# Taking a graph network's transposes off TensorE: VectorE's 32x32 blocks and a way through memory

## The chip, the cores and the metric

One core of one Trainium2 chip. The metric is the time of one execution in device microseconds (us), as the median of several runs.

## The reference, cut to what matters

Thirty-two independent graphs ("batches") of 512 nodes with 128 features pass through four residual layers. Each layer normalizes x, takes ReLU, and adds what a graph layer makes of it.

```python
x   = (32, 512, 128) float32;  adj = (32, 512, 512) float32
h = relu(layernorm(x));  x = x + L0(h)   # degree-normalized aggregation over adj + I
h = relu(layernorm(x));  x = x + L1(h)   # three projections, aggregations over adj and its transpose, update, tanh
h = relu(layernorm(x));  x = x + L2(h)   # four such layers in a row; rows and columns of adj scaled to unit length
h = relu(layernorm(x));  x = x + L3(h)   # one message and a gated update
```

A projection contracts over features and needs h with features on the partitions; a normalization runs over features and needs nodes on the partitions. So each batch turns a 512x128 block round four times: h into hT for L1, h into f0 for L2, L2's result f back into rows (added to x), and h into hT for L3.

## The kernel before

Every operation is put into a plan: an engine, an estimated duration, what it reads and writes. A list scheduler (`Plan.order`) plays the plan through with these estimates and so fixes the order of instructions on each engine. On the chip each engine takes its instructions in that order, and waits only for what it needs. The estimates decide nothing else. About three batches are under way at a time.

```python
PERIOD = 25.0          # a batch is due this much after the one before it (only sets priorities)
SMALL = 8              # how many buffers of each small kind go round
...
class Plan:
    SIGNAL = {"PE": 0.24, "DVE": 0.16, "ACT": 0.17, "POOL": 0.1, "SP": 0.05, "AQ": 0.05}
    ...
    def t_pow(n):      # planned us of a reciprocal root on GpSimd over n columns
        return 0.9 + 0.1 * n
...
        def normed(xin, out_tag, extra=None):
            v8 = buf("v8", (P, 2 * NC)); n = NC
            mv = moments(xin, v8)                 # VectorE; v8 = variance + eps
            if extra: extra(v8); n = 2 * NC       # first norm of a batch: the degrees too, 8 columns
            inv = buf("sc", (P, 3 * NC))
            op("POOL", t_pow(n), lambda: nc.gpsimd.tensor_tensor(inv[:, :n], v8[:, :n], neg_half[:, :n], op=ALU.pow), ...)
            ...
            op("DVE", 0.08, lambda: nc.vector.scalar_tensor_tensor(nb, mv[:, :, 0], -1.0, inv[...], mult, mult), ...)
            for c in range(NC):                   # ScalarE: h = relu(x * inv + nb), four blocks
                op("ACT", ..., lambda c=c: nc.scalar.activation(h[:, c, :], xin[:, c, :], AF.Relu, bias=nb[...], scale=inv[...]), ...)

        def transposed(h, name):                  # three of the four turnings
            ps = plan.bank("t")
            for c in range(NC):
                op("PE", 0.11, lambda c=c: nc.tensor.transpose(ps[:, c*P:(c+1)*P], h[:, c, :], ident), ...)
            hT = buf("s2", name=name)
            op("ACT", t_act(N), lambda: nc.scalar.copy(hT, ps), ...)
            return hT
...
        # layer 0: adj + I, only the diagonal blocks, on GpSimd (two SBUF inputs)
            nc.gpsimd.tensor_tensor(diag[:, k:k+n, :], blocks_of_aT, ident, op=ALU.add)
...
        # layer 2: adj and its transpose times the reciprocal lengths, 8 VectorE instructions of 128x512 per batch
        for s, m in enumerate((aT, a)):
            for c in range(NC):
                op("DVE", 1.0, lambda: nc.vector.tensor_mul(m[:, c, :], m[:, c, :], rows[:, :, s, :]), ...)   # two SBUF inputs
...
        pst = plan.bank("t")                      # the fourth turning
        for c in range(NC):
            op("PE", 0.11, lambda c=c: nc.tensor.transpose(pst[:, c*P:(c+1)*P], f[0][:, c*P:(c+1)*P], ident), ...)
        tt(x3, lambda: nc.vector.tensor_add(x3, x2, pst), ...)
```

## Time and profile before

| | before |
|---|---|
| time, median of 3 | 2416.8 us (2416.28 to 2417.7) |
| span of the profile | 2415.3 us |
| TensorE busy | 99%, 8898 matmuls, 512 of them transposes |
| VectorE / ScalarE / GpSimd busy | 49% / 33% / 12% |

The measure used throughout is the **step**: the time from one TensorE instruction's start to the next one's. Each group of equal matmuls has a median step; count times median, summed, is the floor, what TensorE needs if nothing is ever late (2355.6 us). What the steps have above it is the stall (38.4 us, of which 16.4 between 100 and 2300 us, "mid-run").

### The profile page before, as it was taken

How to read it: one execution, taken by the hardware profiler on the slowest of the kernel's cores; microseconds unless marked ns; L12 is line 12 of the kernel's file. 1: busy time of each engine (PE TensorE's matmuls, PEld its weight loads, DVE VectorE, ACT ScalarE, POOL GpSimd, SP SyncE). 2: the span in 40 equal slices, each digit the busy share in tenths (PEclk: the TensorE clock that was granted, in tenths of full speed). 3: DMA queues.
4: the chain of work that ended last, by engine and by line, in shares of the span. 5: the costliest groups of instructions: out<-in, count | busy, mean ns of one | idle time of the engine just before them, and what ended most of it. 6: DMA issues, size and time to landing. Idle time of an engine off the chain costs nothing.

```text
span 2415.3 us, 23480 instructions
## 1 busy us (share of the span) xinstructions
PE 2379.2 (99%) x8898; PEld 1464.4 (61%) x8898; DVE 1195.2 (49%) x2855; ACT 790.1 (33%) x1719; POOL 299.0 (12%) x218
## 2 busy tenths in 40 slices
PE   6999999999999999999999999999999999999998
PEld 4566566656665665666566656656665666666565
DVE  7445445545445454455554454544555545555423
ACT  5213333333333333333333333333333333333312
POOL 2001111111111111111111111111111111111001
PEclk9999999999999999999999999999999999999999
DMA  6002221022211122210222111222102221122100
GB/s 250 31 1 70 70 70 44 27 70 70 70 50 31 60 70 70 70 44 27 70 70 70 46 32 62 70 70 70 44 27 70 70 70 44 31 66 70 48 5 9
DMA packets 95441, 139.67 MB, mean 58 GB/s; under 512 B 8160, under 2 KB 41312, under 8 KB 95328
## 3 DMA queue, kind: packets, MB, share of 16 engines
q1 hardware_dynamic: 95040, 138.04, 17.4%
q8 instruction: 70, 1.15, 0.2%
q14 instruction: 43, 0.35, 0.0%
q10 hardware_dynamic: 288, 0.13, 0.0%
HBM read 129.64 MB, written 8.52 MB: 57 GB/s over the span
## 4 chain that ended last, share of the span: by engine, by line
PE 86%; DVE 8%; POOL 3%; ACT 2%; issue 0%; DMA 0%; SPq 0%; POOLq 0%; DVEq 0%
PE ps_agg L284 54%; PE ps_sd L284 18%; PE ps_gate L284 7%; PE ps_upd L284 3%; POOL sc L400 3%; PE ps_t L420 2%; DVE rep L524 1%; PE ps_msg L284 1%; PE ps_lin L284 1%; DVE aT L568 1%; DVE bn L384 1%; DVE sd L455 1%; DVE rep L522 1%; ACT h L412 1%; DVE node L517 1%; DVE xr L594 1%
## 5 line engine op out<-in xcount | busy, mean ns | idle before, releaser
L284 PE MATMUL ps_agg<-aT,sd 128*128 128x512 f32 x1024 | 517.1, 592 | 0.0
L284 PE MATMUL ps_agg<-a,sd 128*128 128x512 f32 x1024 | 516.8, 592 | 0.0
L284 PE MATMUL ps_sd<-w_sb,f 128*128 128x256 f32 x1792 | 488.5, 381 | 1.5 <-ACT f L585 0.8
L455 DVE TENSOR_TENSOR sd<-ps_sd,rf_sb 128x512 f32<-128x512 f32 x256 | 176.3, 689 | 557.1 <-PE ps_sd L284 553.8
L284 PEld LDWEIGHTS ps_sd<-w_sb,f 128*128 128x128 f32 x1792 | 325.7, 191 | 206.9 <-issue 179.9
L400 POOL TENSOR_TENSOR sc<-v,neg_half 128x4 f32<-128x4 f32 (+1 forms) x128 | 196.2, 1533 | 1457.6 <-DVE v L387 1015.6
L412 ACT ACTIVATE h<-xr,nb,sc 128x128 f32<-128x128 f32 x384 | 161.4, 484 | 374.8 <-DVE nb L408 374.7
L284 PEld LDWEIGHTS ps_agg<-a,sd 128*128 128x128 f32 x1024 | 185.0, 190 | 108.8 <-issue 99.5
L284 PEld LDWEIGHTS ps_agg<-aT,sd 128*128 128x128 f32 x1024 | 187.4, 191 | 104.4 <-issue 85.2
L585 ACT ACTIVATE f<-ps_agg,cf_sb 128x512 f32<-128x512 f32 x128 | 87.4, 683 | 439.4 <-PE ps_agg L284 439.4
L284 PE MATMUL ps_agg<-f,w_sb 128*128 128x512 f32 x448 | 229.7, 594 | 0.0
L619 DVE TENSOR_TENSOR g<-ps_gate,r_sb 128x512 f32<-128x512 f32 x128 | 83.4, 684 | 128.3 <-PE ps_gate L284 128.3
L568 DVE TENSOR_TENSOR aT<-aT,rows 128x512 f32<-128x512 f32 x128 | 134.9, 1077 | 3.2 <-PE ps_agg L284 3.0
L284 PE MATMUL ps_agg<-aT,rep 128*128 128x512 f32 x256 | 132.8, 600 | 0.5 <-DVE rep L524 0.5
L568 DVE TENSOR_TENSOR a<-a,rows 128x512 f32<-128x512 f32 x128 | 132.1, 1086 | 2.5 <-PE ps_agg L284 2.5
L284 PE MATMUL ps_agg<-a,rep 128*128 128x512 f32 x256 | 130.7, 592 | 0.0
L284 PE MATMUL ps_agg<-aT,msg 128*128 128x512 f32 x256 | 129.8, 592 | 0.0
L284 PEld LDWEIGHTS ps_agg<-f,w_sb 128*128 128x128 f32 x448 | 84.9, 191 | 73.4 <-issue 62.2
L455 DVE TENSOR_TENSOR sd<-ps_sd,r_sb 128x512 f32<-128x512 f32 x64 | 44.3, 691 | 151.2 <-PE ps_sd L284 151.2
L548 ACT ACTIVATE sq<-aT 128x512 f32<-128x512 f32 x128 | 80.6, 630 | 81.1 <-DMA aT<-in_adjt 78.2
L480 POOL TENSOR_TENSOR diag<-aT,ident 128x512 f32<-128x512 f32 (+1 forms) x35 | 41.4, 1182 | 508.7 <-DMA aT<-in_adjt 441.5
L420 PEld LDWEIGHTS ps_t<-ident,h 128*128 128x128 f32 x384 | 51.9, 141 | 84.1 <-ACT h L412 45.1
(94 smaller groups left out, 2751.0 us busy)
## 6 DMA issues: line engine op xcount, KB each, us to landing
aT<-in_adjt SPq DMA_DIRECT2D x63, 1024.0 KB, 7.7
a<-in_adj SPq DMA_DIRECT2D x31, 1024.0 KB, 6.9
rows<-bounce SPq DMA_DIRECT2D x32, 512.0 KB, 4.1
x<-in_x SPq DMA_DIRECT2D x32, 256.0 KB, 6.2
out<-xo SPq DMA_DIRECT2D x30, 256.0 KB, 2.5
raw<-in_raw SPq DMA_DIRECT2D x2, 768.0 KB, 7.5
a<-in_adj SPq DMA_DIRECT2D x4, 256.0 KB, 6.2
aT<-in_adjt SPq DMA_DIRECT2D x4, 256.0 KB, 6.0
```

Source lines behind the costliest of these rows:

```text
L284: op("PE", t_mm(n), lambda: nc.tensor.matmul(out_of(ps.ap()), lhs(), rhs(), start=start, stop=stop), reads, [(ps, part) if part is not Non ...
L384: op("DVE", 0.193, lambda c=c: nc.vector.bn_stats(st.ap()[:, c, :], xin.ap()[:, c, :]), [xin], [(st, {c})])
L400: op("POOL", t_pow(n), lambda: nc.gpsimd.tensor_tensor(inv.ap()[:, :n], v8.ap()[:, :n], neg_half[:, :n], op=ALU.pow), [v8, NH], [(inv, {0})])
L412: op("ACT", t_act(D, 2), lambda c=c: nc.scalar.activation(h.ap()[:, c, :], xin.ap()[:, c, :], AF.Relu, bias=nb.ap()[:, c:c + 1], scale=inv ...
L420: op("PE", 0.11, lambda c=c: nc.tensor.transpose(ps.ap()[:, c * P:(c + 1) * P], h.ap()[:, c, :], ident), [(h, {c}), ID], [(ps, {c})])
L455: op("DVE", t_tt(N), lambda ps=ps, h=h: nc.vector.tensor_add(sd.ap()[:, 2 * h:2 * h + 2, :], ps.ap().rearrange("p (j v) -> p j v", j=2), a ...
L480: nc.gpsimd.tensor_tensor(diag.ap()[:, k:k + n, :], blocks, ident[:, None, :].to_broadcast([P, n, P]), op=ALU.add)
L517: tt(node, lambda: nc.vector.tensor_max(node.ap(), zn.ap(), en.ap()), N, [zn, en])
L548: op("ACT", 0.73, lambda c=c, s=s, m=m: nc.scalar.activation(sq.ap(), m.ap()[:, c, :], AF.Square, accum_out=stat.ap()[:, s * NC + c:s * NC ...
L568: op("DVE", 1.0, lambda m=m, c=c, s=s: nc.vector.tensor_mul(m.ap()[:, c, :].rearrange("p (k n) -> p k n", k=NC), m.ap()[:, c, :].rearrange ...
L585: op("ACT", t_act(N, 1), lambda ps=ps, i=i, f_new=f_new: nc.scalar.activation(f_new.ap(), ps.ap(), AF.Tanh, bias=cf_sb[:, i:i + 1]), [ps, ...
L619: op("DVE", t_tt(N), lambda ps=ps, c=c: nc.vector.tensor_add(g.ap()[:, c, :], ps.ap(), r_sb[:, R_L3_G:R_L3_G + 4 * D]), [ps, RS], [(g, {c})])
```

## The change

The intent is to take 432 of TensorE's 512 transposes away, since TensorE is the bound. In batches 3 to 29 VectorE transposes the 32x32 blocks of the tile, four DMA writes put the blocks at their places in device memory, and one DMA reads the turned tile back. The planner's constants are set anew as well.

```diff
-PERIOD = 25.0
+PERIOD = 30.0
-SMALL = 8
+SMALL = 16
-    SIGNAL = {"PE": 0.24, "DVE": 0.16, "ACT": 0.17, "POOL": 0.1, "SP": 0.05, "AQ": 0.05}
+    SIGNAL = {"PE": 0.2, "DVE": 0.13, "ACT": 0.14, "POOL": 0.0, "SP": 0.05, "AQ": 0.05}
+    LOAD = 0.1                      # and lag() adds LOAD when the next operation is TensorE's
-    plan = Plan(..., {"bank": 1, "s2": 7, "s4": 1, "s8": 1})
+    plan = Plan(..., {"bank": 1, "s2": 7, "s4": 0, "s8": 0})
+        def turned(m, name):
+            blk, mT = buf("s2", rows_shape, "blk"), buf("s2", rows_shape, name)
+            op("DVE", t_tt(N), lambda: nc.vector.transpose(<blk, column blocks swapped>, <m, in 32-column blocks>), [m], [blk])
+            bounce = buf(f"turn_{name}", rows_shape)
+            for k in range(NC):
+                op("SP", 0.4, lambda k=k: away(k), [blk], [(bounce, {k})], kb=64)       # 32 partitions each
+            op("SP", 0.4, lambda: nc.sync.dma_start(mT.ap(), bounce.tile), [bounce], [mT], kb=256)
+            return mT
+        at_ends = b < 3 or b >= B - 2
         def transposed(h, name):
+            if at_ends: <as before>
+            t, hT = turned(h, "turned"), buf("s2", name=name)
+            op("ACT", t_act(N), lambda: nc.scalar.copy(hT..., turned_cols(t)), [t], [hT])
-        op("POOL", 5.5, lambda: <root of the row lengths>, ...)
+        op("POOL", t_pow(2 * NC), lambda: <root of the row lengths>, ...)
-        <fourth turning on TensorE, added to x2 from PSUM>
+        <if at_ends as before, otherwise f4 = turned(f[0], "f4r") and added to x2 from there>
```

More of the change, by code (lines that the diff above doesn't have):

```diff
@@ L142, in lag @@
         queued = o.engine == n.engine and o.engine in self.RESULT
-        return o.us + self.RESULT[o.engine] if queued else o.us + o.land + self.SIGNAL[o.engine]
+        if queued:
+            return o.us + self.RESULT[o.engine]
+        return o.us + o.land + self.SIGNAL[o.engine] + self.LOAD * (n.engine == "PE")
     def order(self):
@@ L235, in gnn_stack @@
     dram = ctx.enter_context(tc.tile_pool(name="dram", bufs=1, space=bass.MemoryType.DRAM))
-    plan = Plan(sb, psum, {"bank": 8, "s2": 32, "s4": 6, "s8": 10}, {"bank": 1, "s2": 7, "s4": 1, "s8": 1})
+    plan = Plan(sb, psum, {"bank": 8, "s2": 32, "s4": 6, "s8": 10}, {"bank": 1, "s2": 7, "s4": 0, "s8": 0})
     w_sb = const.tile([P, W_COLS], F32, name="w_sb")
@@ L415, in normed, with away, turned_cols @@
             return h, inv
-        def transposed(h, name):
-            ps = plan.bank("t")
-            for c in range(NC):
-                op("PE", 0.11, lambda c=c: nc.tensor.transpose(ps.ap()[:, c * P:(c + 1) * P], h.ap()[:, c, :], ident),
-                   [(h, {c}), ID], [(ps, {c})])
-            hT = buf("s2", name=name)
-            op("ACT", t_act(N), lambda: nc.scalar.copy(hT.ap(), ps.ap()), [ps], [hT])
+        def turned(m, name):
+            blk, mT = buf("s2", rows_shape, "blk"), buf("s2", rows_shape, name)
+            op("DVE", t_tt(N), lambda: nc.vector.transpose(
+                blk.ap().rearrange("p b (c r) -> p c b r", c=NC), m.ap().rearrange(
+                    "p c (b s) -> p c b s", b=NC) if len(m.shape) == 3 else m.ap().rearrange("p (c b s) -> p c b s", c=NC, b=NC)),
+               [m], [blk])
+            bounce = buf(f"turn_{name}", rows_shape)
+            def away(k):
+                if bounce.tile is None:
+                    bounce.tile = dram.tile([P, NC, P], F32, name=bounce.name, tag=f"{bounce.kind}_{bounce.slot}", bufs=1)
+                nc.sync.dma_start(bounce.tile[:, k, :].rearrange("(b s) n -> s b n", b=NC), blk.ap()[k * P // NC:(k + 1) * P // NC])
+            for k in range(NC):
+                op("SP", 0.4, lambda k=k: away(k), [blk], [(bounce, {k})], kb=64)
+            op("SP", 0.4, lambda: nc.sync.dma_start(mT.ap(), bounce.tile), [bounce], [mT], kb=256)
+            return mT
+        def turned_cols(mT):
+            return mT.ap().rearrange("p a (c r) -> p c a r", c=NC)
+        at_ends = b < 3 or b >= B - 2
+        def transposed(h, name):
+            if at_ends:
+                ps, hT = plan.bank("t"), buf("s2", name=name)
+                for c in range(NC):
+                    op("PE", 0.109, lambda c=c: nc.tensor.transpose(ps.ap()[:, c * P:(c + 1) * P], h.ap()[:, c, :], ident),
+                       [(h, {c}), ID], [(ps, {c})])
+                op("ACT", t_act(N), lambda: nc.scalar.copy(hT.ap(), ps.ap()), [ps], [hT])
+                return hT
+            t, hT = turned(h, "turned"), buf("s2", name=name)
+            op("ACT", t_act(N), lambda: nc.scalar.copy(hT.ap().rearrange("p (c a r) -> p c a r", c=NC, a=NC), turned_cols(t)), [t], [hT])
             return hT
@@ L551, in program @@
         op("DVE", 0.08, lambda: nc.vector.tensor_scalar_max(stat.ap(), stat.ap(), NORM_EPS * NORM_EPS), [stat], [stat])
-        op("POOL", 5.5, lambda: nc.gpsimd.tensor_tensor(inv.ap(), stat.ap(), neg_half, op=ALU.pow), [stat, NH], [inv])
+        op("POOL", t_pow(2 * NC), lambda: nc.gpsimd.tensor_tensor(inv.ap(), stat.ap(), neg_half, op=ALU.pow), [stat, NH], [inv])
         bounce, rows = buf("bounce", (P, 2 * NC)), buf("s4", (P, P, 2, NC), "rows")
@@ L588, in program @@
             f = {0: [f_new], 1: [f_new, stashed[1]], 2: [f_new, stashed[1], stashed[0]], 3: [f_new]}[i]
-        pst = plan.bank("t")
-        for c in range(NC):
-            op("PE", 0.11, lambda c=c: nc.tensor.transpose(pst.ap()[:, c * P:(c + 1) * P], f[0].ap()[:, c * P:(c + 1) * P], ident),
-               [f[0], ID], [(pst, {c})])
         x3 = buf("s2", rows_shape, "xr")
-        tt(x3, lambda: nc.vector.tensor_add(flat(x3), flat(x2), pst.ap()), N, [x2, pst])
+        if at_ends:
+            pst = plan.bank("t")
+            for c in range(NC):
+                op("PE", 0.109, lambda c=c: nc.tensor.transpose(pst.ap()[:, c * P:(c + 1) * P], f[0].ap()[:, c * P:(c + 1) * P], ident),
+                   [f[0], ID], [(pst, {c})])
+            tt(x3, lambda: nc.vector.tensor_add(flat(x3), flat(x2), pst.ap()), N, [x2, pst])
+        else:
+            f4 = turned(f[0], "f4r")
+            tt(x3, lambda: nc.vector.tensor_add(
+                x3.ap().rearrange("p c (a r) -> p c a r", a=NC), x2.ap().rearrange("p c (a r) -> p c a r", a=NC), turned_cols(f4)),
+               N, [x2, f4])
         h3, _ = normed(x3, "h")
```

## The prediction

> **What bounds the kernel now.** I read the page first: the busy times, the row of 40 slices, the chain that ended last.
>
> ```profile
> span 2415.3 us, 23480 instructions
> ...
> PE 2379.2 (99%) x8898; PEld 1464.4 (61%) x8898; DVE 1195.2 (49%) x2855; ACT 790.1 (33%) x1719; POOL 299.0 (12%) x218
> ...
> PE   6999999999999999999999999999999999999998
> ...
> PEclk9999999999999999999999999999999999999999
> ...
> PE 86%; DVE 8%; POOL 3%; ACT 2%; issue 0%; DMA 0%; SPq 0%; POOLq 0%; DVEq 0%
> ```
>
> TensorE is full in every slice but the first and the last, at full clock, and it holds 86% of the chain. VectorE is half idle. But a busy PE can hide small stalls, since each matmul's duration contains its pipeline. So I took the steps from one matmul's start to the next, as the timeline in mid-run shows them:
>
> ```profile
> 1199.95 0.38 PE L420 MATMUL ps_t<-ident,h 128*128 128x128 f32 x2
> 1200.17 1.02 PE L284 MATMUL ps_agg<-aT,msg 128*128 128x512 f32 x2
> 1201.03 1.02 PE L284 MATMUL ps_agg<-aT,sd 128*128 128x512 f32 x2
> 1201.89 1.03 PE L284 MATMUL ps_sd<-w_sb,f 128*128 128x256 f32 x4
> 1202.75 1.02 PE L284 MATMUL ps_agg<-aT,msg 128*128 128x512 f32 x2
> ```
>
> Two transposes hold the array for 0.22 us, two matmuls of 512 columns for 0.86, four of 256 for 0.86. The medians of these steps over the trace are 0.429 us for 512 columns, 0.323 for 384, 0.216 for 256, 0.111 for 128, and 0.109 for a transpose. With the counts of the groups by form (3328, 128, 2688, 2745 of 128 columns) the sum, each group at its own median, is 2355.6 us of unavoidable TensorE time. The rest of the 2415.3 is: 11.2 before the first matmul, 10.1 after the start of the last, and 38.4 of steps longer than their medians. Of those 38.4, 19.6 fall into the first 100 us, 16.4 between 100 and 2300, 2.0 after, and the rest is rounding. So 97.5% of the span is pure TensorE occupancy. Only shortening that, or those 60 us, can help.
>
> The transposes, in the groups by form:
>
> ```profile
> L420 PE MATMUL ps_t<-ident,h 128*128 128x128 f32 x384 | 70.4, 276 | 6.1 <-ACT h L412 5.8
> L591 PE MATMUL ps_t<-ident,f 128*128 128x128 f32 x128 | 24.2, 273 | 0.2 <-ACT f L585 0.2
> ```
>
> 512 of them, 16 for each of the 32 batches. The trap is the 276 ns mean: times 432 it would promise 119 us. The occupancy is the 0.109 step, as the timeline shows.
>
> What stalls there are in mid-run stand in the view of waits:
>
> ```profile
> PEld ps_upd L284 <- ACT agg_out L533: 14.1, 26, 0.6
> ```
>
> In steps, that wait costs 10.1 us over 25 batches (about 0.4 each), and the first aggregation over rep about 0.13 per batch. This is a loss of the plan, not of the transposes.
>
> **What the skill says.** The Trainium skill, "TensorE: Matmul & The Clock Gate", Part 4: PE-mode transpose, gives about 275 ns for a transpose within a kernel, mostly access latency, and output to PSUM. The trace agrees on duration (276), but back to back only 109 ns are occupied. "VectorE: DVE Perf Modes", The three transpose paths: VectorE transposes 32x32 blocks only, so moving the blocks has to be done by something else; that is what the way through memory is for. "Vector Engine (DVE) Microarchitecture Reference", 3.8: the transposing array is pipelined to one element per cycle and lane. The trace before has no such instruction, so I price it like another one-element-per-cycle pass over 512 columns, the adds at 0.69 us. "DMA: Bandwidth & Descriptors", Anatomy of one DMA: a fixed cost near 2 us per transfer. The trace has less: 1.4 us for 4 KB.
>
> **The change part by part.**
>
> Removed: in batches 3 to 29, 27 x 16 = 432 transposes. 432 x 0.109 = 47.1 us of TensorE time, all of it on the bound. The order of instructions confirms that no matmul is added. The weight loads of those transposes run beside matmuls and are worth nothing more.
>
> Added on VectorE: 4 block transposes per batch, 108 x 0.69 = 75 us (an estimate from the adds). VectorE goes from 1195 to about 1270 us, 54% of the shorter span. It stays off the bound. ScalarE's 81 copies stay, now out of SBUF instead of PSUM: some 0.63 us as its other SBUF passes, instead of 0.586; 81 x 0.045 = 4 us, beside everything.
>
> Added on the queue: per turning, four writes of 64 KB and one read of 256 KB, 540 transfers and 108 x 0.5 MB = 57 MB on top of 140. The page says the engines are busy for 17.4% of the span. At the same time per packet (95,040 packets over 0.174 x 16 x 2415 us is 71 ns each), the added 55,296 + 13,824 packets take 4.9 ms of 38.6, so 13% more: about 30%. Not a bound. How long one turning takes I read from the DMA issues:
>
> ```profile
> out<-xo SPq DMA_DIRECT2D x30, 256.0 KB, 2.5
> ...
> out<-xo SPq DMA_DIRECT2D x8, 64.0 KB, 1.6
> ```
>
> 0.69 (blocks) + 3 further issues of about 0.45 on the queue + 1.6 (last write) + 2.5 (read back) = 6.1 us, instead of 4 x 0.109 plus pipeline, about 0.7. That is 5.4 us more, four times in a batch's chain: 22 us of latency per batch.
>
> Is the latency hidden? The kernel interleaves about three batches, so what counts is how much TensorE work stands in the order between the last matmul a chain hangs on and the first that needs its result. I counted this along the changed kernel's order, matmuls at their steps, the chain at durations of the trace before. With the figures above for turnings, mid-run slack is about 21 us for the first layer's hT, some 18 us or more for the last layer's, and 6.6 us or more at the tightest of the second layer's f0 (apart from one early batch at 2.3). A batch now stretches over 242 us of TensorE work in the order instead of 202, which pays for the latency. The tightest links are elsewhere: sd into the aggregation and f1, f2 into their projections, near zero (-0.2 to +0.2), where before it was rep (-0.3) and hT (0.0).
>
> Moved: the planner's constants (0.1 us more ahead of TensorE, the reciprocal root at 1.7 instead of 5.5 us, where the trace has 1663 ns), more small buffers, no s4 and s8 slots held back. The agg_out link that cost 0.4 per batch now has about 1.2 us of slack in place of 0.3, and rep 1.1. So most of the 16.4 us of mid-run stalls should go, and new ones will come at the sd, f1 and f2 links or where VectorE's and ScalarE's queues stand behind a late transfer. I put the new sum at 10 us: -6.
>
> Ends: the first batches and the last two keep TensorE's transposes. The last 60 us of TensorE's order are the same, instruction by instruction. The first 45 us differ little; one chain is tighter by about 1 us: +1.
>
> Sum: 2416.8 - 47.1 - 6 + 1 = 2364.7; I say 2365, -2.1%.
>
> **The rivals.**
>
> First, the wait changes place. VectorE and ScalarE take instructions in order; the add of f4r and the copies of hT wait for a transfer, and behind them stand the sd additions that TensorE needs, with 2.4 us of median slack. The read of f4r is issued behind a 1 MB load. If reads come 1 to 2 us late, TensorE loses perhaps 1 us per batch, 27 us in all, and the time is near 2385 to 2390. For it: the single in-order queue, where transfers wait on semaphores. Against it: the queue had almost no queueing waits before, and the order already leaves a 1 MB load over 4 us before the read behind it.
>
> Second, only the occupancy counts and stalls stay as they are (16 us): 2370, -1.95%, just on the near side of the line.
>
> Third, the new plan is better than I credit and stalls in mid-run fall to 2 or 3 us: 2356, -2.5%.
>
> Fourth, the block transposes on 4-byte data are twice as slow (1.3 us). VectorE would be at 58%, still no bound, but sd would be late more often: plus 5 to 15 us.
>
> **Range and chances.** The 47.1 us are firm to within 1. What is open is the stall sum, from 2 to 30 us, which makes 2356 to 2385; I take 2352 to 2384. The line of 2% lies at 2368.5, so my middle is only 3.5 us inside it. Second, first and fourth rival are on the far side; third and my sum on the near one. Faster 0.57, same 0.39, slower 0.04: to be slower by 2% would need 95 us of new stalls, 3.5 us per batch, which the slack speaks against.
>
> **What would show it right or wrong.** Right: 80 transposes left on TensorE; PE still 99% in the middle slices; the steps unchanged at 0.429 and 0.216; the agg_out wait gone; VectorE near 1270 us and the block transposes near 0.69 us; DMA share about 30%; landing of the writes below 3 us, of the reads near 2.5 to 4. Wrong: a repeated gap on TensorE in each batch (some 72 us apart) that ends with sd, f or hT, with VectorE or ScalarE in turn idle until the landing of turned or f4r; or block transposes far longer than the adds; or steps of matmuls grown longer beside the DMA traffic.

## More of the kernel before

```profile
L400 POOL TENSOR_TENSOR sc<-v,neg_half 128x4 f32<-128x4 f32 x96 | 143.8, 1498 | 1004.1 <-DVE v L387 1004.0
L400 POOL TENSOR_TENSOR sc<-v,neg_half 128x8 f32<-128x8 f32 x32 | 52.4, 1638 | 453.6 <-DVE v L471 438.4 <-DVE v L387 11.7 <-DVE sc L405 3.5
```

The mean of the 4-column root is 1498 ns, its median in the trace 1009. A mean half above the median says that some of the 96 are much longer: 143.8 - 96 x 1.009 is 46.9 us, which is 27 roots that take 2.72 us instead of 1.01.

## The result, and the profile after

| | before | after |
|---|---|---|
| time, median of 4 | 2416.78 us (2416.28 to 2417.7) | 2386.68 us (2385.3 to 2387.39) |
| span of the profile | 2415.3 | 2385.2 |
| floor of TensorE's steps | 2355.6 | 2308.7 |
| stalls: first 100 us | 19.6 | 23.7 |
| stalls: mid-run | 16.4 | 29.9 |
| stalls: last 115 us | 2.0 | 2.1 |
| 4-column roots (`sc`) on GpSimd over 2 us | 27 of 96 | 26 of 96 |
| 8-column roots (`sc`) over 2 us | 0 of 32 | 25 of 32 |
| VectorE's `nb` over 1 us | 0 of 128 | 29 of 128 |

The ratio is 0.9874 (95% interval 0.9857 to 0.9891). Ratios here are the mean time of one kernel's runs over that of the other's runs of the same rounds, so not quite the ratio of the medians quoted. The change gained 30.1 us where 51.8 were predicted (2416.8 to 2365), and it lies outside the range of 2352 to 2384.

The page of the kernel after, busy times and chain:

```profile
PE 2338.4 (98%) x8466; PEld 1427.9 (60%) x8466; DVE 1298.3 (54%) x2963; ACT 792.4 (33%) x1719; POOL 352.7 (15%) x218
...
PE 70%; DVE 13%; POOL 7%; ACT 3%; DMA 3%; issue 2%; SPq 1%; POOLq 0%; ACTq 0%; DVEq 0%
```

There are 432 matmul instructions fewer, VectorE is busier by 103 us, and the DMA queue holds 25.6% of the engines. But GpSimd, which got no new instruction, is busier by 54 us, and its share of the chain that ended last rose from 3% to 7%, while TensorE's fell from 86% to 70%.

The way through memory, from the DMA view of the kernel after (transfer, count, KB each, median us from issue to landing):

```profile
turn_turned<-blk SPq DMA_DIRECT2D x324, 64.0 KB, 1.8
turned<-turn_turned SPq DMA_DIRECT2D x81, 256.0 KB, 2.6
...
f4r<-turn_f4r SPq DMA_DIRECT2D x27, 256.0 KB, 5.5
```

From the start of the block transpose to the landing of the read it is 6.55 us in the median for hT and f0, where 6.1 was predicted, and 11.5 us for f4r, whose read sits behind a 1 MB load.

Where TensorE waits now, from the view of waits (engine and line that wait, what for: us in total, times, longest):

```profile
PEld ps_sd L288 <- ACT f L619: 13.7, 25, 0.8
...
PE ps_sd L288 <- ACT f L619: 8.0, 22, 0.4
...
PEld ps_upd L288 <- ACT agg_out L567: 11.5, 23, 0.5
```

Part of a weight load's wait is hidden behind the matmul that still runs, so these sums are not stalls. In steps, a batch in mid-run now loses 0.63 us where L2's third layer projects f2, the second layer's result (`ps_sd<-w_sb,f`), 0.19 at an aggregation over sd and 0.06 at `agg_in`: 0.88 per batch, 24 us in mid-run. (The text for run 1 says the second layer. But the matmuls behind this wait project two inputs, f2 and f1, which only the third layer has.) Before it lost 0.40 at `agg_out` and 0.13 at the aggregation over rep. So the old stall left its place, and a larger one came at another.

GpSimd's roots in the groups by form, after:

```profile
L404 POOL TENSOR_TENSOR sc<-v,neg_half 128x4 f32<-128x4 f32 x96 | 142.1, 1480 | 1316.1 <-DVE v L391 1308.6 <-DVE mv L390 5.2 <-DVE nb L412 2.0
L404 POOL TENSOR_TENSOR sc<-v,neg_half 128x8 f32<-128x8 f32 x32 | 108.7, 3397 | 649.1 <-DVE v L391 602.8 <-DVE stat L585 37.5 <-DVE v L505 8.8
```

The 8-column root went from 1638 to 3397 ns though nothing about it was changed. One stall of 0.63 us, from its cause on, in the timeline of the kernel after (us from the span's start, duration, engine, line, instruction; in brackets the wait ahead of it):

```profile
1318.35 0.17 DVE L391 TENSOR_SCALAR v<-mv 128x4 f32<-128x4 f32 x1
1318.42 1.08 DVE L602 TENSOR_TENSOR aT<-aT,rows 128x512 f32<-128x512 f32 x1
...
1318.66 2.72 POOL L404 TENSOR_TENSOR sc<-v,neg_half 128x4 f32<-128x4 f32 x1 [4.46 <-DVE v L391]
...
1319.42 1.08 DVE L602 TENSOR_TENSOR a<-a,rows 128x512 f32<-128x512 f32 x1
...
1321.41 0.16 DVE L412 SCALAR_TENSOR_TENSOR nb<-mv,sc 128x4 f32<-128x4 f32 x1 [0.91 <-POOL sc L404]
...
1321.61 1.66 ACT L416 ACTIVATE h<-xr,nb,sc 128x128 f32<-128x128 f32 x4 [1.53 <-DVE nb L412]
...
1323.17 0.67 ACT L619 ACTIVATE f<-ps_agg,cf_sb 128x512 f32<-128x512 f32 x1
...
1323.89 1.56 PE L288 MATMUL ps_sd<-w_sb,f 128*128 128x256 f32 x6 [0.36 <-ACT f L619]
```

The root is released at 1318.66, while VectorE is in the first of two multiplications with `rows`, each with two inputs from SBUF. The second ends at 1320.50, and the root ends 0.88 us later. A root takes 1.01 us alone, so nearly all its work came after the multiplications. `nb` needs the root, ScalarE's four h need `nb`, and ScalarE's tanh, which makes this f (f2), stands behind those four in its order. f had waited for no input (no bracket); it was only in a late queue. TensorE starts the projection 0.63 us late.

The Trainium skill, "SBUF — State Buffer", section "SBUF: two separate sides", has a mechanism that fits: VectorE and GpSimd share a pair of ports as an exclusive lock, which a VectorE instruction with two SBUF inputs takes against a GpSimd instruction that reads SBUF; "whichever … starts first gets the pair for the whole instruction; the other fully blocks." The prediction didn't look there. The trace agrees in three ways: roots beside multiplications take 2.72 us; roots beside VectorE work with one input from PSUM are not held (1.02 us at 55.87 us of this trace, beside `z<-ps_lin`); and the lock works the other way too, as the same timeline shows 30 us earlier, where VectorE's `nb`, an instruction on 4 columns, takes 1.21 us beside GpSimd's addition of the diagonal:

```profile
1288.19 1.26 POOL L514 TENSOR_TENSOR diag<-aT,ident 128x512 f32<-128x512 f32 x1
...
1288.25 1.21 DVE L412 SCALAR_TENSOR_TENSOR nb<-mv,sc 128x4 f32<-128x4 f32 x1 [1.19 <-POOL sc L404]
```

And the stall of the kernel before, which the prediction called a loss of the plan, has the same cause:

```profile
1331.99 2.09 DVE L568 TENSOR_TENSOR aT<-aT,rows 128x512 f32<-128x512 f32 x2
...
1332.24 2.72 POOL L400 TENSOR_TENSOR sc<-v,neg_half 128x4 f32<-128x4 f32 x1 [12.20 <-DVE v L387]
...
1334.99 0.16 DVE L408 SCALAR_TENSOR_TENSOR nb<-mv,sc 128x4 f32<-128x4 f32 x1 [0.91 <-POOL sc L400]
...
1335.19 0.49 ACT L412 ACTIVATE h<-xr,nb,sc 128x128 f32<-128x128 f32 x1 [0.67 <-DVE nb L408]
1335.59 0.56 ACT L533 COPY agg_out<-ps_agg 128x512 f32<-128x512 f32 x1
...
1336.21 0.49 PE L284 MATMUL ps_upd<-w_sb,agg_out 128*128 128x128 f32 x2
```

There the held root delays one h, behind which stands the copy of `agg_out`.

### The profile page after: what moved, and what is told of

Read it like the earlier page. It is cut to its first block, busy times and chain, and to the rows that moved or that the text cites. A ratio compares the mean times of both kernels' runs of the same rounds, so it can differ in the third digit from the quotient of the medians. Undisturbed runs are those within 1.5% of the kernel's fastest.

```text
span 2385.2 us, 23873 instructions
## 1 busy us (share of the span) xinstructions
PE 2338.4 (98%) x8466; PEld 1427.9 (60%) x8466; DVE 1298.3 (54%) x2963; ACT 792.4 (33%) x1719; POOL 352.7 (15%) x218
## 3 DMA queue, kind: packets, MB, share of 16 engines
q1 hardware_dynamic: 172800, 194.70, 25.6%
## 4 chain that ended last, share of the span: by engine, by line
PE 70%; DVE 13%; POOL 7%; ACT 3%; DMA 3%; issue 2%; SPq 1%; POOLq 0%; ACTq 0%; DVEq 0%
PE ps_agg L288 44%; PE ps_sd L288 16%; POOL sc L404 7%; PE ps_gate L288 6%; ACT h L416 2%; DVE aT L602 2%; DVE sd L489 2%; DVE bn L388 2%; PE ps_lin L288 1%; DVE a L602 1%; PE ps_msg L288 1%; DVE rep L558 1%; PE ps_upd L288 1%; SPq L434 1%; DMA turned<-turn_turned 1%
## 5 line engine op out<-in xcount | busy, mean ns | idle before, releaser
L404 POOL TENSOR_TENSOR sc<-v,neg_half 128x4 f32<-128x4 f32 (+1 forms) x128 | 250.8, 1960 | 1965.1 <-DVE v L391 1911.5
L288 PE MATMUL ps_agg<-a,sd 128*128 128x512 f32 x1024 | 496.9, 592 | 0.0
L288 PE MATMUL ps_sd<-w_sb,f 128*128 128x256 f32 x1792 | 482.6, 382 | 8.6 <-ACT f L619 8.0
L288 PEld LDWEIGHTS ps_sd<-w_sb,f 128*128 128x128 f32 x1792 | 333.4, 191 | 234.7 <-issue 198.0
L503 DVE TENSOR_REDUCE stat<-a 128x4 f32<-128x2048 f32 (+1 forms) x35 | 73.5, 2102 | 142.0 <-DMA a<-in_adj 141.9
L602 DVE TENSOR_TENSOR a<-a,rows 128x512 f32<-128x512 f32 x128 | 138.4, 1085 | 3.8 <-PE ps_agg L288 3.8
L288 PE MATMUL ps_agg<-aT,h 128*128 128x256 f32 (+2 forms) x384 | 109.0, 381 | 0.0
L412 DVE SCALAR_TENSOR_TENSOR nb<-mv,sc 128x4 f32<-128x4 f32 x128 | 50.8, 397 | 95.5 <-POOL sc L404 95.2
L642 DVE TENSOR_TENSOR msg<-ps_msg,r_sb 128x512 f32<-128x512 f32 x32 | 22.1, 690 | 146.4 <-PE ps_msg L288 146.4
L425 DVE STREAM_TRANSPOSE blk<-h 128x512 f32<-128x512 f32 x81 | 57.6, 711 | 68.3 <-ACT h L416 68.3
```

Source lines behind the costliest of these rows:

```text
L288: op("PE", t_mm(n), lambda: nc.tensor.matmul(out_of(ps.ap()), lhs(), rhs(), start=start, stop=stop), reads, [(ps, part) if part is not Non ...
L404: op("POOL", t_pow(n), lambda: nc.gpsimd.tensor_tensor(inv.ap()[:, :n], v8.ap()[:, :n], neg_half[:, :n], op=ALU.pow), [v8, NH], [(inv, {0})])
L412: op("DVE", 0.08, lambda: nc.vector.scalar_tensor_tensor(nb.ap(), mv.ap()[:, :, 0], -1.0, inv.ap()[:, at:at + NC], op0=ALU.mult, op1=ALU.m ...
L425: op("DVE", t_tt(N), lambda: nc.vector.transpose(blk.ap().rearrange("p b (c r) -> p c b r", c=NC), m.ap().rearrange("p c (b s) -> p c b s" ...
L503: op("DVE", t_tt(n * N), lambda s=s: nc.vector.tensor_reduce(stat.ap()[:, s], a.ap()[:, s, :], AX.X, ALU.add), [(a, set(range(NC)[s]))], [ ...
L602: op("DVE", 1.0, lambda m=m, c=c, s=s: nc.vector.tensor_mul(m.ap()[:, c, :].rearrange("p (k n) -> p k n", k=NC), m.ap()[:, c, :].rearrange ...
```

## The experiments

**Theory P** (ports): the missing 22 us are mainly stalls from GpSimd's roots and VectorE's two-input instructions holding each other up, at places where the new order has no room. **Rivals**: the way through memory makes ScalarE or VectorE late (the prediction's first rival, "theory L" in the texts); the planner's new constants plan links too tightly; or the turnings as such disturb the order.

Every result is the median of 4 runs, with the ratio to the kernel before in the same rounds. That kernel's medians were 2416.99, 2416.42 and 2416.65 us in the three sets of rounds, so results of different sets may be compared to some tenths of a us.

### 1. After, without roots on GpSimd

Each of the 160 roots becomes one VectorE instruction of the same shape at the same place in the order. Its output is wrong, which doesn't matter for the time.

```diff
-nc.gpsimd.tensor_tensor(inv[:, :n], v8[:, :n], neg_half[:, :n], op=ALU.pow)
+nc.vector.tensor_scalar(inv[:, :n], v8[:, :n], 1e-6, 0.3, op0=ALU.mult, op1=ALU.add)
```

> The changed kernel with its 160 reciprocal roots on GpSimd replaced, in the same place of the order, by one small VectorE instruction (a linear stand-in: the result is wrong on purpose). Theory P (the stalls of TensorE in mid-run come from GpSimd and VectorE waiting for each other[...]): the stall of 0.63 us per batch ahead of the second layer's projection of f goes, and most of the 0.19 ahead of the aggregation with aT; mid-run stalls fall from 29 us to under 12, the time from 2386.7 to 2362 to 2372, and no VectorE instruction of 4 columns is longer than 0.4 us except beside the diagonal's addition. Theory L (the stalls come from the longer way through memory): mid-run stalls stay at 25 us or more, since no transfer is touched; the time is within 4 us of 2386.7.

Measured: 2363.04 us, ratio 0.9776 (0.9762 to 0.9791), 23.6 less than the changed kernel. Mid-run stalls fell from 29.9 to 10.4. The 0.63 per batch at `ps_sd` is gone, the 0.19 at the aggregation stays, and the transfers are all still there. So the transfers don't make the 0.63. It was also expected that most of the 0.19 would go; it didn't. This run takes away the root's own microsecond as well as the hold, so it doesn't yet tell those two apart; runs 8 and 9 do. It ends the hold of `nb` too (0 of 128 over 1 us), which run 6 prices by itself.

### 2. Before, without roots on GpSimd

The same edit in the kernel before.

> The same stand-in in the kernel before (wrong result on purpose). Theory P: its mid-run stalls (0.40 us per batch ahead of the update's agg_out, 0.13 ahead of the aggregation over rep) come from the same hold, seen as a root of 2.72 us instead of 1.01; the agg_out part goes, the time falls by 8 to 15 us to 2402 to 2409. Theory L says nothing of this kernel, which has no way through memory; if the time stays within 3 us of 2416.8, P is wrong for the kernel before.

Measured: 2404.35 us, ratio 0.9948 (0.9933 to 0.9963). The 0.40 per batch at `agg_out` is gone, the 0.13 over rep stays, mid-run stalls went from 16.4 to 3.7. The kernel before already paid 12.6 us for its roots.

### 3. The constants alone

TensorE's transposes in all batches, everything else as after.

```diff
-        at_ends = b < 3 or b >= B - 2
+        at_ends = True
```

> The changed kernel's planner constants (period, signal times, load time, root time, small buffers, slots) with TensorE's transposes in all batches: the other part of the change alone. If the constants by themselves are good (my prediction's claim that they save about 6 us): 2408 to 2412. If the constants cost what was lost (17 us of stalls): 2425 to 2435. If the loss comes only with the turnings: within 3 us of 2416.8.

Measured: 2462.27 us, ratio 1.0187 (1.0172 to 1.0203): 45 us slower than before. None of the three ranges holds it. Mid-run stalls are 59.2, some 2 us per batch, at the transposes of h and the projection behind them. The timeline of this kernel shows the chain:

```profile
1309.02 1.26 POOL L514 TENSOR_TENSOR diag<-aT,ident 128x512 f32<-128x512 f32 x1
1309.08 1.22 DVE L412 SCALAR_TENSOR_TENSOR nb<-mv,sc 128x4 f32<-128x4 f32 x1 [1.18 <-POOL sc L404]
...
1310.34 1.65 ACT L416 ACTIVATE h<-xr,nb,sc 128x128 f32<-128x128 f32 x4 [4.55 <-DVE nb L412]
...
1310.88 1.48 PE L452 MATMUL ps_t<-ident,h 128*128 128x128 f32 x4 [0.44 <-ACT h L416]
```

`nb` is held by the diagonal's addition, h is late, and TensorE then takes four transposes at the pace at which ScalarE makes h, 0.38 us each in place of 0.11.

### 4. The turnings alone

The way through memory with the old constants.

```diff
-PERIOD = 30.0;  SMALL = 16;  LOAD = 0.1;  kept s4 0, s8 0;  new SIGNAL;  root of the row lengths t_pow(8)
+PERIOD = 25.0;  SMALL = 8;   LOAD = 0.0;  kept s4 1, s8 1;  old SIGNAL;  root of the row lengths 5.5
```

> The turnings by VectorE and memory with the planner constants of the kernel before: the first part of the change alone. The floor is the same as that of the changed kernel (2308.7 us of TensorE steps). If the constants help: 2390 to 2405, slower than the changed kernel. If they hurt: 2366 to 2380. Theory P expects roots longer than 2.5 us on GpSimd wherever TensorE stalls in mid-run; theory L expects TensorE's gaps to end with hT or f copied from a turned tile, or xr that waited for f4r.

Measured: 2435.49 us, ratio 1.0073 (1.0056 to 1.009): 18.5 us slower than before, with 84.7 us of mid-run stalls, and outside both expected ranges. Only 11 of the 96 4-column roots are over 2 us, so theory P doesn't explain this kernel's stalls. Their chief shape is TensorE with nothing left to do between a layer's last aggregation and the next layer's projection:

```profile
1331.29 3.60 PE L288 MATMUL ps_agg<-a,sd 128*128 128x512 f32 x8
...
1334.92 0.69 ACT L619 ACTIVATE f<-ps_agg,cf_sb 128x512 f32<-128x512 f32 x1 [4.43 <-PE ps_agg L288]
...
1335.66 0.70 PE L288 MATMUL ps_sd<-w_sb,f 128*128 128x256 f32 x2 [0.78 <-ACT f L619]
```

A batch stretches over 202 to 224 us of TensorE work in this order, where after has 242, and run 3's order 198. So a batch is spread wide only by both parts together. That the old constants leave too little work of other batches at hand to cover the longer chain is argued from this and not tested. The two parts don't add: +45 and +18.5 us alone, -30 together. Without the turnings the new constants only hurt. Which of the six constants matters was not tried.

### 5. The way through memory made longer

The read-back is issued twice, one after the other.

```diff
-            op("SP", 0.4, lambda: nc.sync.dma_start(mT.ap(), bounce.tile), [bounce], [mT], kb=256)
+            def back():
+                for _ in range(2): nc.sync.dma_start(mT.ap(), bounce.tile)
+            op("SP", 0.4, back, [bounce], [mT], kb=256)
```

> The changed kernel where each turned tile is read back from memory twice, the second read after the first: 108 transfers of 256 KB more, and every way through memory about 2.6 us longer; the order of all else is the same, the result right. Theory P ([...]the way is hidden by the slack in the order, 6 us or more): within 5 us of 2386.7. Theory L (the latency of the way sets TensorE's stalls): at 4 turnings a batch the stalls rise by several tenths of a us per batch at least, 27 x 2.6 = 70 us at the most; I would take it as shown from 2400 on.

Measured: 2490.73 us, ratio 1.031 (1.0295 to 1.0326), 104 us more than the changed kernel. The expectation, at most 5 us, was wrong, and by the line (2400 and more) theory L would count as shown. But the run tests a longer way than the changed kernel has; that its stalls of 0.63 don't come from the way is seen in runs 1, 9 and 11, which keep it as it is. The view of the tile f4r shows the add that uses it (its three durations are least, median and most) and its waits:

```profile
L636 DVE TENSOR_TENSOR xr<-xr,f4r x27: 691/693/694, 381.1 to 2362.6; 128x512 f32<-128x512 f32 x27
...
  DMA f4r<-turn_f4r: 39.4, 27
```

VectorE waits for f4r in 27 of 27 batches, 1.46 us each. In the changed kernel it waits 1.5 us in all, and f4r lands a median 1.5 us ahead of its use. So at its real length the way of f4r is hidden, but with less than one more read to spare. The 6.6 us of slack in the prediction counted TensorE's work up to the first matmul that needs the result. An engine on the way that takes its instructions in order can have its own, smaller slack: everything behind the waiting add waits with it. VectorE's 39.4 us are not the whole of the 104. ScalarE's copies of turned tiles waited 464 us for their reads in place of 192, and TensorE's largest stalls stand ahead of `agg_in` (42.5 us) and of the projection of f0, itself a turned tile (28.5). How the 104 us divide isn't shown.

### 6. The diagonal's addition on VectorE

After, with the GpSimd instruction that holds `nb` moved. The planned order is unchanged.

```diff
-            nc.gpsimd.tensor_tensor(diag..., blocks, ident..., op=ALU.add)
+            nc.vector.tensor_tensor(diag..., blocks, ident..., op=ALU.add)
```

> The changed kernel with the diagonal's addition (32 instructions of 1.27 us on GpSimd) on VectorE in the same place of the order. Right result. It takes away the other direction of the hold: the scale-times-mean instruction of 4 columns that lasts 1.22 us in 26 batches. My reading after the first experiments: in the changed kernel this delay falls on a turning, whose slack swallows it, so the time stays within 4 us of 2386.7, and the instruction falls to 0.16 us. If it sat on TensorE's path, 5 to 25 us would be saved.

Measured: 2382.11 us, ratio 0.9859 (0.9842 to 0.9875): 4.6 us less (at most 4 were expected), 3.1 of them in the first 100 us. `nb` is back at 0.17 us or less. The hold in this direction is real in the timeline, but worth little in this order.

### 7. The constants alone, with the diagonal's addition on VectorE

Runs 3 and 6 together.

> The constants-only kernel (2462.3 us, TensorE's transposes) with the diagonal's addition on VectorE. There the delayed instruction stands directly before TensorE's transposes, which wait about 2.0 us per batch. If the hold by the diagonal's addition is the cause: 1.06 us per batch, so 25 to 35 us less, 2427 to 2437. If the stall is only a tight plan: within 5 us of 2462.

Measured: 2440.47 us, ratio 1.01 (1.0085 to 1.0115): 21.8 us less than run 3, where 25 to 35 were expected. About half of run 3's loss is the hold; the rest is the tight plan and a new 0.27 us per batch ahead of the aggregation over sd.

### 8. The multiplications out of the way, put in one block

After; each multiplication with `rows` that stands between a root's input and its use goes directly behind that use. The instructions and their engines stay, and the result is right.

```diff
-        for o in plan.order():
+        for o in apart(plan.order()):      # moves only nc.vector.tensor_mul(m, m, rows) on VectorE
```

> The changed kernel, same instructions on the same engines, right result; only on VectorE's order the multiplications with rows (two SBUF inputs, 1.08 us) are moved from between a reciprocal root's input and its first use to just after that use. Theory P: the roots fall from 2.72 and 3.96 us to 1.0 and 1.64, the 0.63 us stall per batch goes as in the kernel with the stand-in, the time is 2362 to 2374. Theory L, or if the stand-in gained only because a hop between engines went: within 4 us of 2386.7.

Measured: 2379.92 us, ratio 0.985 (0.9835 to 0.9864): 6.8 us less, not the 13 to 25 expected. The hold is gone (4-column roots 1011 ns in the mean), and so is the 0.63. But up to seven multiplications in a row now keep VectorE from other work, and 0.42 us per batch appear ahead of the aggregation with aT.

### 9. The two multiplications set aside

As run 8, but only the multiplications beside the 4-column roots move, to behind the next norm and three instructions further. The result is right.

> The changed kernel, right result, same instructions on the same engines; the two multiplications with rows per batch that stand on VectorE between the input of the root of the last layer's norm and its use go behind the next norm, three instructions further, where TensorE's work has slack. Unlike the kernel that moved them only just behind the use (2379.9, where a new stall of 0.42 us per batch came ahead of the aggregation with aT), nothing urgent stands behind them. Theory P: the root falls from 2.72 to 1.01 us, the 0.63 us per batch go and nothing comes in their place: 2366 to 2374. If the gain of the stand-in was due to the missing hop between engines: 2380 or more.

Measured: 2374.2 us, ratio 0.9821 (0.9805 to 0.9838): 12.5 us less than after, 0.2 outside the expected 2366 to 2374. The roots in this kernel's groups by form:

```profile
L435 POOL TENSOR_TENSOR sc<-v,neg_half 128x4 f32<-128x4 f32 x96 | 97.0, 1011 | 1347.7 <-DVE v L422 1340.2 <-DVE mv L421 5.2 <-DVE nb L443 2.1
```

The same place in the batch as in the timeline of after:

```profile
1311.40 1.01 POOL L435 TENSOR_TENSOR sc<-v,neg_half 128x4 f32<-128x4 f32 x1 [4.46 <-DVE v L422]
...
1312.44 0.16 DVE L443 SCALAR_TENSOR_TENSOR nb<-mv,sc 128x4 f32<-128x4 f32 x1 [1.18 <-POOL sc L435]
1312.52 1.09 DVE L633 TENSOR_TENSOR a<-a,rows 128x512 f32<-128x512 f32 x1
...
1312.72 1.65 ACT L447 ACTIVATE h<-xr,nb,sc 128x128 f32<-128x128 f32 x4
...
1314.98 0.69 ACT L650 ACTIVATE f<-ps_agg,cf_sb 128x512 f32<-128x512 f32 x1 [0.62 <-PE ps_agg L319]
```

The root takes 1.01 us, and f now waits for its own input (the bracket) and not for ScalarE's queue. Mid-run stalls are 17.2 instead of 29.9: 12.7 us less, as much as the time fell. This is the cleanest test of theory P: nothing left out, nothing moved to another engine, only the neighbours in time. One rival remains: the two multiplications, 2.1 us, also stood ahead of `nb` in VectorE's own order, hold or no hold. Run 1 settles it. At the 26 places where both stand between `v` and `nb`, `nb` starts a median 3.07 us after `v` in the changed kernel, and 2.14 in run 1, where both still stand there, and the 0.63 is gone all the same. So their own time alone doesn't make the stall.

### 10. Run 9 with the diagonal's addition on VectorE

> The same with the diagonal's addition on VectorE, which by itself saved 4.6 us, 3 of them in the first 100 us. If the two savings are separate: 2362 to 2370, and every stall of mid-run other than the planned tight link from sd to the aggregation (0.19 us per batch) is gone.

Measured: 2370.36 us, ratio 0.9807 (0.9793 to 0.9822), 16.3 us less than after, beside 12.5 + 4.6 from runs 9 and 6: here the two directions of the hold nearly add. It is 0.4 us outside the expected 2362 to 2370. Some 15 us of mid-run stalls are left, 8.7 of them at the aggregation over sd, the tight link that the text names.

### 11. After, with the planner told of the hold

The planned duration of a root gets the 1.7 us that the hold adds. The result is right.

```diff
     def t_pow(n):
-        return 0.9 + 0.1 * n
+        return 2.6 + 0.1 * n
```

> The changed kernel whose planner is told that a root takes 1.7 us more (3.0 and 3.4 us instead of 1.3 and 1.7), so that it lays out the whole order anew with room for the hold; right result. If the planner only lacked the hold: 2364 to 2376. The order changes everywhere, so a miss says little.

Measured: 2363.07 us (2362.81 to 2363.39), ratio 0.9778 (0.9763 to 0.9792). It beats both kernels: 23.6 us less than after by one constant, as much as taking the roots out altogether (run 1), and 0.9 below the expected 2364 to 2376. In the groups by form the roots are still held:

```profile
L404 POOL TENSOR_TENSOR sc<-v,neg_half 128x8 f32<-128x8 f32 x32 | 133.7, 4179 | 1301.8 <-DVE v L391 1185.1 <-DVE stat L585 107.0 <-DVE v L505 8.6
L404 POOL TENSOR_TENSOR sc<-v,neg_half 128x4 f32<-128x4 f32 x96 | 100.5, 1047 | 682.1 <-DVE v L391 590.9 <-DVE nb L412 78.5 <-PE ps_msg L288 12.8
```

The hold has moved to the 8-column roots (4.97 us in the median), and mid-run stalls are 7.9 us in all. So a hold need not cost much. It costs where an engine that TensorE depends on has no slack. The 8-column roots can cost little here even at 4179 ns, so the row that showed the largest rise after the change is not by itself the loss.

### 12. Run 11 with the diagonal's addition planned and run on VectorE

> The same room for roots, and the diagonal's addition planned and run on VectorE. 2360 to 2375 if both work together; the planner's new order makes this the least certain of the four.

Measured: 2373.65 us, ratio 0.9822 (0.9807 to 0.9837), correct and inside the wide range, but 10.6 us worse than run 11. Every edit that the planner sees makes a new order; this one has 17.3 us of mid-run stalls. What helped after (run 6) doesn't help here.

## Why the prediction was wrong

The direction was right (faster). The size was not: -1.24% instead of -2.1%. By the steps of the prediction:

- **Removed occupancy**: 47.1 us predicted, 46.9 measured. 80 transposes are left, and the steps per form are unchanged. Right.
- **Added work on VectorE**: block transposes 711 ns where 690 was estimated, VectorE 1298 us where 1270 was said. The difference is about what `nb` adds: its 128 instructions take 50.8 us in place of 21.0. The fourth rival, block transposes twice as slow, is ruled out by the 711.
- **DMA**: a share of 25.6% where 30% was estimated. The profile counts 77,760 packets more, not 69,120 (8,640 of them are under 512 B), but these took 39 ns each in the mean, not 71. The way took 6.55 us where 6.1 was estimated, and the reads of f4r landed after 5.5 us, not 2.5 to 4. The way is hidden at its real length. But "6.6 us or more" of slack was counted at TensorE alone; run 5 shows that the nearest in-order engine has less than one read (2.6 us).
- **The failing step** is "I put the new sum at 10 us: -6". Mid-run stalls rose by 13.5 us to 29.9. The step rested on reading the `agg_out` wait as "a loss of the plan", which a new plan could only improve. It was a root on GpSimd that VectorE's multiplications held up for 1.71 us (in run 2 the roots cost 12.6 us, their own time included). The planner of the change knew nothing of the hold either. In its order the held root stands ahead of f, where it costs 0.63 per batch in place of 0.40 (run 9 gives 12.7 us of the 19.5 by which the term was wrong). Most of the rest is the 0.19 per batch at the aggregation over sd, about 5 us in 27 batches. It stays in runs 1 and 9, so neither this hold nor the roots make it. The prediction had named it, and f2's way into the projection, among the tightest links (-0.2 to +0.2 us of slack), but left both in one guessed sum; and f2's was late by the hold, which the plan's estimates lacked.
- **Ends**: "+1" was +4.1 us in the first 100 us. Run 6 takes 3.1 us of this stretch's stalls away, so it is mainly the diagonal's addition; the rest stays open.
- **The rivals**: the first gave 2385 to 2390, which is the measured time, but by luck. The shape was near: an in-order engine comes late, and TensorE waits for it in L2, though at the projection of f2 and not mainly at the sd additions that the rival named. The cause was wrong. It blamed late reads, while ScalarE was late through the hold; runs 1, 9 and 11 keep every transfer and lose the 0.63.

In sum, from the prediction's 2364.7 to 2386.7, to 0.1 us: 19.5 us mid-run and 3.2 at the ends, less 0.8 of rounding in the steps and plus 0.2 of occupancy. The mid-run stalls in the range went up to 30 us, so 29.9 was just inside it; the time fell outside since the ends came on top.

Shown by runs: the hold and its cost of 12.5 us (run 9), and that room in the plan wins back 23.6 (run 11). Run 11 gains 11 us more than run 9. Its order spreads a batch over 255 us of TensorE work where after has 242. Which of its shifts in the order bring the 11 us is open, as is which planner constant makes run 3 slow.

## What to carry to other kernels

When work is taken off the bounding engine, the freed time is only worth what the new order doesn't give back: for every in-order engine, not only the bound, ask how much room stands ahead of each instruction that something else can hold up. A group whose mean lies well above its median (here 1498 against 1009 ns) has two kinds of instances; find what stands beside the long ones before calling its waits a loss of the plan. Where VectorE instructions with two SBUF inputs and GpSimd instructions can meet, give the planner the held duration, or keep them apart, and check that what is moved doesn't block the engine elsewhere.

## What the Trainium skill lacked or had wrong

- "SBUF — State Buffer", section "SBUF: two separate sides": it has the lock, but not that a waiting GpSimd instruction doesn't get it between back-to-back VectorE instructions. A root released 0.24 us into one multiplication waited for the next one also (2.72 us in place of 1.01); 8-column roots took 3.95 us in the median in the changed kernel and 4.97 in run 11, in place of 1.64.
- No page has the duration of a reciprocal root by `pow` on GpSimd: 1.01 us for 128x4, 1.64 us for 128x8, when not held.
- "TensorE: Matmul & The Clock Gate", Part 4: it gives a transpose's duration, not its occupancy. Back to back, fp32 transposes of 128x128 step by 109 ns at 276 ns each, and the occupancy is what removing them is worth: 46.9 us for 432.
- "VectorE: DVE Perf Modes", The three transpose paths: the table has 128x128 bf16 only. A 128x512 fp32 transpose in 32x32 blocks took 711 ns, about the time of an add of the same size (690).
